# A two-transformer kernel on one core: the first transformer's query lengths moved from the queries to the score rows

## Chip, core and metric

One core of a Trainium2 chip runs the whole program. The metric is the time of one execution on the device in microseconds (us); the median of three runs is given, and beside it one execution that the hardware profiler recorded.

## What is computed

Four blocks in a row, each `x = x + s * silu(f)`, where `s` is an attention-like function and `f` a feed-forward-like function of the normalised `x`. The third block's `f` is a small transformer of six layers (below, the first transformer: 16 heads of 64, window 32); the fourth block's is another of two layers (8 heads, window 64). The tokens are 4 rows of 512, the width is 128, all in f32. Cut to what matters, a layer of the first transformer is:

```python
q, k, v = split(shift_tokens(x) @ Wqkv)          # 16 heads of 64
q = q / max(norm(q), 1e-12) * qs                 # per token and head
k = k / max(norm(k), 1e-12) * ksc
q = q * cos * scale + rotate_half(q) * sin * scale
k = k * cos / scale + rotate_half(k) * sin / scale
sim = einsum(q, k of this window and the one before) * 8, masked
x = softmax(sim) @ v @ Wo + x
x = feed_forward(layernorm(shift_tokens(x))) + x
```

The length of a query is one number per token and head. It can be applied to the query before the scores, or to the finished row of scores.

## The kernel before

Everything lies transposed: 128 channels on the partitions, tokens along the free axis. `_Transformer` runs three generators side by side, `queries_keys`, `attention` and `feed_forward`. The main loop (L724 to L732) takes one slot after the other; a slot is one batch row and one group of 8 heads, so the first transformer has 6 x 4 x 2 = 48 slots, and a few more to fill and drain. In a slot, `merge` (L949) takes turns between the generators by the costs that they yield (in us, written by hand: 10.3 for a slot of queries and keys, 20.4 for one of attention, 7.7 and 1.7 in turn for feed-forward). What comes out is then put in order on each engine by the framework's scheduler; each engine works through its own list in order.

**Queries and keys** (L1278). For queries (i = 0) and then keys (i = 1), and for two groups g of four heads, two 512-column products fill one PSUM tile S (L1300). From S come the squares (L1304, ScalarE), their sum over two halves (L1305, GpSimd), the two products with the rotation tables (L1306 and L1308, VectorE) and the sum of these (L1309, GpSimd). `unit_length` (L1319) sums the squares over a head by a product with a matrix of ones (L1326), takes Ln and Exp on ScalarE in place (L1329, L1330), and VectorE multiplies the rotated tile by the result (L1333, 128x1024, once per g). Eight DMAs on SP's queue (L1340) stack the tile by head pairs. Both queries and keys go through `unit_length`.

**Attention** (L1495) works on units: four heads (j = 0 or 1) of a slot's eight, all 512 tokens, so two units a slot. `values` (L1343) projects 64 tokens at a time into column halves (16 products of 256 columns a slot, L1358), copies them out of PSUM (L1365), and four DMAs (L1369, L1371) copy them to `ve`, shifted by a window for every other block. `scores` (L1383) writes the mask and adds 64 small products of 64 rows, 32 columns of weights and 64 moving columns (L1402), in two parts with the `turn` of the unit before in between. VectorE takes the maximum of each row (L1415) and subtracts it (L1419, two instructions), ScalarE takes the exponential (L1424), VectorE the row sums and their reciprocals (L1426, L1428). `turn` (L1431) transposes the exponentials (8 transpositions, copied by L1440). `weigh` (L1443) has 64 small products with the values, and VectorE divides by the row sums (L1473). `turn_back` (L1484) transposes the result (copies L1493), and four products with Wo (L1529) are added to the stream by L1533.

**Feed-forward** (L1543): layernorm (L1550 to L1559), products up (L1566, L1567), Gelu (L1569, with a load of its table), the gated product (L1571), products down (L1578). It takes two slots per row, so slots with the layernorm and the down products alternate with slots with the up products, roughly.

All of these share one PSUM pool of four S tiles (L715, `ps`), which is all of PSUM. A product into a tile waits until the last reader of the tile that had this place is done.

## Time and profile before

| | us |
|---|---|
| median of three runs | 3872.96 (3869.68 to 3877.02) |
| span of the profiled execution, first to last instruction | 3866.4 |
| first transformer in it | about 1640 to 3300 |
| TensorE busy in the span | 3490.9 |
| VectorE | 2476.9 |
| ScalarE | 1847.0 |
| GpSimd | 1161.2 |

For the profiled execution only its span is at hand, 6.6 us below the median of the runs. Engines are named PE (TensorE), PEld (its weight loads), DVE (VectorE), ACT (ScalarE), POOL (GpSimd), SPq (the DMA queue of SyncE). A group's line gives the source line, the engine, the operation, output and inputs with their shapes, the count, then busy time and mean ns of one, then the idle time before them and who ended it. A line of the timeline has start, duration, engine, line, operation and count, with the wait in brackets where there was one. A matrix product in f32 leaves two records. L122 and L126 are the helpers that issue products and transpositions, so groups under them are told apart by their tiles: `hb,l_wqk` is the query and key projection, `sqp,l_k` the product with ones, `hb,l_wv` or `l_wv,hb` the values, `l_v.,l_PT` the weighing, `l_OT,l_wo` the output projection, `core,l_P` and `core,l_On` the two transpositions.

### The profile page before, as it was taken

How to read it: one execution, taken by the hardware profiler on the slowest of the kernel's cores; microseconds unless marked ns; L12 is line 12 of the kernel's file. 1: busy time of each engine (PE TensorE's matmuls, PEld its weight loads, DVE VectorE, ACT ScalarE, POOL GpSimd, SP SyncE). 2: the span in 40 equal slices, each digit the busy share in tenths (PEclk: the TensorE clock that was granted, in tenths of full speed). 3: DMA queues.
4: the chain of work that ended last, by engine and by line, in shares of the span. 5: the costliest groups of instructions: out<-in, count | busy, mean ns of one | idle time of the engine just before them, and what ended most of it. 6: DMA issues, size and time to landing. Idle time of an engine off the chain costs nothing.

```text
span 3866.4 us, 105326 instructions
## 1 busy us (share of the span) xinstructions
PE 3490.9 (90%) x46789; PEld 1892.2 (49%) x46917; DVE 2476.9 (64%) x3429; ACT 1847.0 (48%) x2508; POOL 1161.2 (30%) x994
## 2 busy tenths in 40 slices
PE   6886999899899999899999999999999999778887
PEld 4554455444444443454555555555555555445444
DVE  6675555411553351677888888888888887367765
ACT  3333666623133334455555555555555555445555
POOL 1001344400021113443443443443443342042220
PEclk7677999999899999999999999999999999889998
DMA  1000000001000000444334444444444434322221
GB/s 39 8 24 24 8 1 1 1 30 52 2 1 3 3 1 2 116 99 117 95 94 122 96 96 120 95 99 117 98 99 103 103 88 98 110 63 69 53 49 42
DMA packets 123574, 236.12 MB, mean 61 GB/s; under 512 B 29624, under 2 KB 44128, under 8 KB 117728
## 3 DMA queue, kind: packets, MB, share of 16 engines
q1 hardware_dynamic: 114064, 209.58, 22.1%
q10 hardware_dynamic: 8624, 19.29, 1.6%
q8 instruction: 369, 6.05, 0.7%
q0 software_dynamic: 432, 0.51, 0.1%
q14 instruction: 85, 0.70, 0.1%
HBM read 50.08 MB, written 5.54 MB: 14 GB/s over the span
## 4 chain that ended last, share of the span: by engine, by line
PE 69%; ACT 11%; DVE 9%; issue 6%; DMA 2%; POOL 2%; SPq 0%; DVEq 0%; POOLq 0%; ACTq 0%
PE S L122 45%; PE S L126 6%; PE M L122 5%; PE S L1402 4%; PE o L1104 4%; ACT l_P L581 3%; PE o L614 2%; ACT l_PT L1440 1%; DMA l_tab<-in_k_rot_l 1%; PE S L1014 1%; DVE l_mx L1079 1%; ACT l_P L1126 1%; DVE l_rot L1333 1%; PE M L741 1%; DVE l_rot L1306 1%
## 5 line engine op out<-in xcount | busy, mean ns | idle before, releaser
L1309 POOL TENSOR_TENSOR l_rot<-l_rot,rotp 128x1024 f32<-128x1024 f32 x224 | 527.5, 2364 | 285.9 <-DVE rotp L1308 219.2
L1305 POOL TENSOR_TENSOR sqp<-sqp 128x512 f32<-128x512 f32 x224 | 293.3, 1310 | 832.8 <-ACT sqp L1304 825.6
L122 PE MATMUL S<-hb,l_wqk 128*128 128x512 f32 x896 | 449.4, 621 | 36.7 <-ACT l_PT L1440 11.2
L1304 ACT ACTIVATE sqp<-S 128x1024 f32<-128x1024 f32 x224 | 229.5, 1025 | 319.2 <-PE S L122 318.0
L1333 DVE SCALAR_TENSOR_TENSOR l_rot<-S,l_rot 128x1024 f32<-128x1024 f32 x224 | 262.9, 1211 | 65.3 <-ACT S L1330 37.4
L1306 DVE TENSOR_TENSOR l_rot<-S,l_tab 128x1024 f32<-128x1024 f32 x224 | 272.1, 1215 | 50.0 <-ACT sqp L1304 46.6
L126 PE MATMUL S<-core,l_P 128*128 128x128 f32 x1856 | 265.2, 287 | 38.9 <-ACT l_P L1424 16.4
L126 PEld LDWEIGHTS S<-core,l_P 128*128 128x128 f32 x1856 | 215.0, 146 | 136.8 <-issue 45.8
L122 PE MATMUL S<-l_KT,l_QT 32*128 32x256 f32 (+7 forms) x1536 | 247.4, 475 | 34.7 <-ACT l_P L1126 14.5
L1126 ACT ACTIVATE l_P<-S 128x1024 f32<-128x1024 f32 x160 | 156.8, 1023 | 254.9 <-PE S L122 254.1
L1308 DVE TENSOR_TENSOR rotp<-S,l_tab 128x1024 f32<-128x1024 f32 x224 | 270.5, 1208 | 1.4 <-POOL l_rot L1309 1.3
L122 PEld LDWEIGHTS S<-hb,l_wqk 128*128 128x128 f32 x896 | 158.3, 192 | 224.7 <-issue 151.6
L122 PE MATMUL S<-sqp,l_k 128*128 128x512 f32 x448 | 226.5, 623 | 19.1 <-issue 7.2
L1402 PE MATMUL S<-l_qk 64*32 64x64 f32 (+1 forms) x13312 | 221.1, 230 | 19.4 <-DMA l_qk<-l_rot 1.9
L1079 DVE TENSOR_REDUCE l_mx<-S 128x2 f32<-128x768 f32 (+1 forms) x192 | 154.9, 863 | 123.8 <-PE S L1014 123.8
L1402 PEld LDWEIGHTS S<-l_qk 64*32 64x32 f32 (+1 forms) x13312 | 168.2, 108 | 134.0 <-issue 129.6
L1130 POOL TENSOR_SCALAR_AFFINE_SELECT l_P<-l_P 128x256 f32<-128x256 f32 x256 | 99.8, 408 | 405.5 <-ACT l_P L1126 398.5
L122 PE MATMUL S<-l_wv,hb 128*64 128x256 f32 (+1 forms) x1600 | 219.1, 395 | 2.4 <-ACT l_vo L1365 1.2
L122 PE MATMUL S<-l_OT,l_wo 128*128 128x512 f32 (+1 forms) x512 | 207.1, 544 | 8.0 <-DVE ffu L1571 7.9
L1415 DVE TENSOR_REDUCE mx<-S 128x16 f32<-128x1024 f32 (+1 forms) x128 | 155.7, 1216 | 89.9 <-PE S L1402 89.8
L122 PE MATMUL S<-hb,l_w 128*128 128x512 f32 (+1 forms) x384 | 189.6, 630 | 23.5 <-DVE hb L1559 14.1
L122 PEld LDWEIGHTS S<-l_ve,l_PT 64*32 64x32 f32 (+1 forms) x6656 | 159.9, 108 | 99.2 <-issue 70.5
(360 smaller groups left out, 6544.8 us busy)
## 6 DMA issues: line engine op xcount, KB each, us to landing
l_qk<-l_rot SPq DMA_DIRECT2D x896, 128.0 KB
l_ve<-l_vo SPq DMA_DIRECT2D x112, 256.0 KB
l_ve<-l_vo SPq DMA_DIRECT2D x96, 224.0 KB
l_tab<-in_k_rot_l ACTq DMA_DIRECT2D x16, 1024.0 KB
l_wqk<-in_l2Wqkv SPq DMA_DIRECT2D x12, 512.0 KB
l_wv<-in_l2Wqkv SPq DMA_DIRECT2D x12, 256.0 KB
l_wo<-in_l2Wo SPq DMA_DIRECT2D x12, 256.0 KB
l_ve<-l_vo SPq DMA_DIRECT2D x24, 128.0 KB
```

The costliest lines, as they stand in the source:

```text
L122: self.nc.tensor.matmul(out, lhsT, rhs, start=start, stop=stop)
L126: self.nc.tensor.transpose(out, in_, self.ident[:n, :n])
L1079: nc.vector.tensor_reduce(mxv[:, bs, 2 * m + e, 3 - i], s[u][:, :, c : c + n], axis=AX.X, op=ALU.max)
L1126: nc.scalar.activation(P[u], s[u], AF.Exp, scale=scale)
L1304: nc.scalar.activation(sq, p, AF.Square)
L1305: nc.gpsimd.tensor_tensor(sq[:, 0, :], sq[:, 0, :], sq[:, 1, :], ALU.add)
L1306: nc.vector.tensor_tensor(t[:, g], p, tab[:, 0], ALU.mult)
L1308: nc.vector.tensor_tensor(m, p, tab[:, 1], ALU.mult)
L1309: nc.gpsimd.tensor_tensor(t[:, g], t[:, g], m[:, ::-1, :], ALU.add)
L1333: nc.vector.scalar_tensor_tensor(t[:, g], p[:, g, :].unsqueeze(1).to_broadcast([128, 2, S]), 1e12, t[:, g], ALU.min, ALU.mult)
L1402: net.nc.tensor.matmul(sv[W * bl : W * bl + W, e, t, g, :].rearrange("p (s k) -> p s k", s=2), qk[0][r, g, j, W * c : W * c + W], kw, star ...
L1415: nc.vector.tensor_reduce(mx, flat, axis=AX.X, op=ALU.max)
```

## The change

The first transformer (window 32) gets a class of its own, `_Paired`; the second keeps `_Transformer`.

- Keys are projected before queries. Keys still go through `unit_length`. Queries are stacked unscaled, right after their rotation.
- `lengths` sums the query squares on tokens: 32 products per slot, each with 128x32 squares as weights and 4 columns of the ones matrix moving, into a 128x32 result; Ln and Exp on that, and a small minimum on GpSimd.
- `weights_of`: maximum, one subtraction for the whole unit (128x1024), and then GpSimd multiplies the unit's rows by the query lengths; the exponential comes after that, in `exponentials`.
- The row sums and reciprocals move into `turn`, after the copy of the transposed exponentials.
- The 64 score products, and the 64 weighing products of the unit before, stand in one run each, with nothing yielded in between.
- Values are projected 128 tokens at a time over all 512 columns (4 products a slot); the blocks of a unit are numbered otherwise (c = 4(2t + bl/2) + 2a + bl%2), and the mask, the weights' column order and the copies to `ve` (again four DMAs) go with it.
- `turn_back` copies once (128x1024) in place of two halves, and the stream is added in two halves of 256 columns.
- A unit's order of work: its scores, weighing of the unit before, then values or output projection, then both transpositions; the attention weight of a slot is 16.1 in place of 20.4.

```diff
-            t = _Transformer(self, pre, heads, window, pools, consts)
+            t = (_Paired if window == 32 else _Transformer)(self, pre, heads, window, pools, consts)
...
-        self.attention_weight = 20.4 if self.split else 25.0
+        self.attention_weight = 16.1 if self.split else 25.0
...
+                for i in (1, 0):
...
+                        sq = self.TP.tile([128, 2, S], F32, name="sqp", bufs=3)
+                        nc.scalar.activation(sq, p, AF.Square)
+                        nc.gpsimd.tensor_tensor(sq[:, 0, :], sq[:, 0, :], sq[:, 1, :], ALU.add)
+                        nc.vector.tensor_tensor(t[:, g], p, tab[:, 0], ALU.mult)
+                        m = self.TP.tile([128, 2, S], F32, name="rotp", bufs=2)
+                        nc.vector.tensor_tensor(m, p, tab[:, 1], ALU.mult)
+                        nc.gpsimd.tensor_tensor(t[:, g], t[:, g], m[:, ::-1, :], ALU.add)
+                        sums.append(sq)
+                        if before:
+                            made["k"] = yield from self.unit_length(*before)
+                            before = None
+                    before = sums, t
+                made["q"] = self.stack(t)
+                made["r"] = yield from self.lengths(sums)
...
+    def lengths(self, sums):
+        net, nc = self.net, self.nc
+        p = self.M()[:, 0:32]
+        pv = p.rearrange("p (h n) -> p h n", h=4)
+        for t in range(2):
+            for g in range(2):
+                for a in range(2):
+                    for bl in range(4):
+                        c = 4 * (2 * t + bl // 2) + 2 * a + bl % 2
+                        net.mm(
+                            pv[32 * bl : 32 * bl + 32, :, 4 * t + 2 * g + a], sums[g][:, 0, 32 * c : 32 * c + 32], self.ones[:, ::32]
+                        )
+        yield 0.8
+        r = net.stat(32, "rq")
+        nc.scalar.activation(r, p, AF.Ln, bias=self.tiny)
+        nc.scalar.activation(r, r, AF.Exp, scale=-0.5)
+        nc.gpsimd.tensor_scalar(r, r, 1e12, None, ALU.min)
+        return r
...
+        for m in (0, 2):
+            p = self.S2()
+            for n in range(2):
+                net.mm(p[:, n, :], hb[:, 128 * (m + n) : 128 * (m + n) + 128], w)
+            yield 1.72
+            nc.scalar.copy(vo[:, m : m + 2, :], p)
+        for lo in (0, 64):
+            nc.sync.dma_start(ve[lo : lo + 32], vo[lo : lo + 32])
+        nc.sync.dma_start(ve[96:128], vo[32:64])
+        nc.sync.dma_start(ve[32:64, 1:4, :], vo[96:128, 0:3, :])
...
+    def weights_of(self, u, s, r):
+        net, nc = self.net, self.nc
+        mx = net.stat(16, "mx")
+        sv = s.rearrange("p e (n k) -> p (e n) k", k=64)
+        nc.vector.tensor_reduce(mx, sv, axis=AX.X, op=ALU.max)
+        P = u["P"] = self.PP.tile([128, 16, 64], F32, name=self.pre + "_P")
+        nc.vector.tensor_tensor(P, sv, mx.unsqueeze(2).to_broadcast([128, 16, 64]), ALU.subtract)
+        rq = r[:, 16 * u["j"] : 16 * u["j"] + 16]
+        nc.gpsimd.tensor_tensor(P, P, rq.unsqueeze(2).to_broadcast([128, 16, 64]), ALU.mult)
+
+    def exponentials(self, u):
+        self.nc.scalar.activation(u["P"], u["P"], AF.Exp, scale=8.0)
+
+    def turn(self, u):
...
+        u["PT"] = self.PP.tile([128, 8, 128], F32, name=self.pre + "_PT")
+        nc.scalar.copy(u["PT"], t)
+        rs = net.stat(16, "rs")
+        nc.vector.tensor_reduce(rs, P, axis=AX.X, op=ALU.add)
+        u["r"] = net.stat(16, "r")
+        nc.vector.reciprocal(u["r"], rs)
...
+            if u:
+                if i % 2 == 0:
+                    qk = self.made.pop((u["l"], u["b"], u["gp"]))
+                else:
+                    u["ve"], u["vo"] = last["ve"], last["vo"]
+                s = self.scores(qk, u["j"])
+            if last:
+                o = self.weigh(last)
+            if u:
+                self.weights_of(u, s, qk["r"])
+            if last:
+                self.divide(last, o)
+            if u or last:
+                yield 2.8
+            behind = None
+            if i % 2 == 0 and i + 2 < len(units):
+                behind = self.values(units[i + 2])
+            elif i % 2 and i > 2:
+                behind = self.close(units[i - 2], OT.pop(i - 2))
+            if behind:
+                yield next(behind)
+            if u:
+                self.exponentials(u)
+            if behind:
+                yield from behind
+            if last:
+                if i % 2:
+                    made = self.TP.tile([128, 4, S], F32, name=self.pre + "_OT", bufs=1)
+                else:
+                    OT[i - 1] = made
+                self.turn_back(last, made)
+                yield 0.9
+            if u:
+                self.turn(u)
+                yield 0.9
```

More of the change, by code (lines that the diff above doesn't have):

```diff
@@ L1201, in __init__ @@
         nc.vector.tensor_copy(self.identb, net.ident)
-        self.ve = [C.tile([128, self.NU, 1024 // self.NB], F32, name=f"{pre}_ve{i}") for i in range(2)]
-        for i in range(2 if self.split else 1):
+        self.ve = [C.tile([128, 4 if self.split else 2, 512], F32, name=f"{pre}_ve{i}") for i in range(2)]
+        if not self.split:
             for lo, hi in self.second():
-                nc.gpsimd.memset(self.ve[i][lo:hi, 0, :], 0.0)
+                nc.gpsimd.memset(self.ve[0][lo:hi, 0, :], 0.0)
         self.made, self.shift, self.weights = {}, {}, {}
-        self.attention_weight = 20.4 if self.split else 25.0
+        self.attention_weight = 16.1 if self.split else 25.0
         self.feed_forward_weights = (7.7, 1.7) if self.GP == 2 else (9.4,)
@@ L1335, in unit_length, with stack @@
             )
+        return self.stack(t)
+    def stack(self, t):
+        nc = self.nc
         out = self.QK.tile([128, 2, 2, S], F32, name=self.pre + "_qk")
@@ L1581, in feed_forward, with __init__, queries_keys, values @@
             yield None
+class _Paired(_Transformer):
+    def __init__(self, *args):
+        super().__init__(*args)
+        for ve in self.ve:
+            self.nc.gpsimd.memset(ve[32:64, 0, :], 0.0)
+    def queries_keys(self, rows):
+        net, nc = self.net, self.nc
+        for l, b in rows:
+            hb = net.shifted(net.tok(self.y, b), self.TP, 3)
+            self.shift[l, b] = hb
+            hk = hb.rearrange("p (u s k) -> p s u k", s=2, k=self.W)
+            for gp in range(self.GP):
+                w = self.part("qk", l, gp)
+                before, made = None, {}
+                for i in (1, 0):
+                    tab = self.tables(l, i)
+                    t = self.TP.tile([128, 2, 2, S], F32, name=self.pre + "_rot", bufs=2)
+                    sums = []
+                    for g in range(2):
+                        p = self.S2()
+                        for h in range(2):
+                            c = 128 * (4 * g + 2 * i + h)
+                            o = p[:, h, :]
+                            net.mm(
+                                o.rearrange("p (s u k) -> p s u k", s=2, k=self.W) if i else o, w[:, c : c + 128],
+                                hk if i else hb,
+                            )
[14 more added lines that the diff above has]
+                made["r"] = yield from self.lengths(sums)
+                self.made[l, b, gp] = made
+                yield None
+    def lengths(self, sums):
[3 more added lines that the diff above has]
+        for t in range(2):
+            for g in range(2):
+                for a in range(2):
+                    for bl in range(4):
+                        c = 4 * (2 * t + bl // 2) + 2 * a + bl % 2
+                        net.mm(
+                            pv[32 * bl : 32 * bl + 32, :, 4 * t + 2 * g + a], sums[g][:, 0, 32 * c : 32 * c + 32], self.ones[:, ::32]
+                        )
+        yield 0.8
[4 more added lines that the diff above has]
+        return r
+    def values(self, u):
+        net, nc = self.net, self.nc
+        w, hb = self.part("v", u["l"], u["gp"]), self.shift[u["l"], u["b"]]
+        ve = u["ve"] = self.ve[u["gp"]]
+        vo = u["vo"] = self.VP.tile([128, 4, 512], F32, name=self.pre + "_vo")
+        for m in (0, 2):
+            p = self.S2()
+            for n in range(2):
+                net.mm(p[:, n, :], hb[:, 128 * (m + n) : 128 * (m + n) + 128], w)
+            yield 1.72
+            nc.scalar.copy(vo[:, m : m + 2, :], p)
[3 more added lines that the diff above has]
+        nc.sync.dma_start(ve[32:64, 1:4, :], vo[96:128, 0:3, :])
+    def scores(self, qk, j):
+        net, nc = self.net, self.nc
+        s = self.S2()
+        for e in range(2):
+            net.mm(s[:, e, :], self.identb, self.mask[:, 0, :])
+        sv = s.rearrange("p e (t g a s k) -> p e t g a s k", t=2, g=2, a=2, s=2)
+        for t in range(2):
+            for g in range(2):
+                for a in range(2):
+                    for bl in range(4):
+                        c = 4 * (2 * t + bl // 2) + 2 * a + bl % 2
+                        k0, step = self.window(c)
+                        for e in range(2):
+                            r = slice(64 * e, 64 * e + 64)
+                            kt = qk["k"][r, g, j, :]
+                            kw = bass.AP(kt.tensor, kt.offset + k0, [list(kt.ap[0]), [step, 2], [1, 32]])
+                            nc.tensor.matmul(
+                                sv[32 * bl : 32 * bl + 32, e, t, g, a], qk["q"][r, g, j, 32 * c : 32 * c + 32], kw,
+                                start=False, stop=True, skip_group_check=True, tile_position=(r.start, 32 * bl),
+                            )
+        return s
+    def weights_of(self, u, s, r):
+        net, nc = self.net, self.nc
+        mx = net.stat(16, "mx")
[8 more added lines that the diff above has]
+    def turn(self, u):
+        net, nc = self.net, self.nc
+        P = u["P"]
+        t = self.S2().rearrange("p a (b q) -> p (a b) q", q=128)
+        for i in range(8):
+            net.transpose(t[:, i, :], P[:, 2 * i : 2 * i + 2, :].rearrange("p a k -> p (a k)"))
+        u["PT"] = self.PP.tile([128, 8, 128], F32, name=self.pre + "_PT")
[4 more added lines that the diff above has]
+        nc.vector.reciprocal(u["r"], rs)
+    def weigh(self, u):
+        net = self.net
+        PT, vo, ve, j = (u[k] for k in ("PT", "vo", "ve", "j"))
+        o = self.S2()
+        for t in range(2):
+            for g in range(2):
+                for e in range(2):
+                    d = 64 * (4 * g + 2 * j + e)
+                    x = 64 * (4 * t + 2 * g + e)
+                    for bl in range(4):
+                        v = vo if bl % 2 else ve
+                        for a in range(2):
+                            r = slice(64 * a, 64 * a + 64)
+                            net.mm(
+                                o[32 * bl : 32 * bl + 32, a, x : x + 64], PT[r, 4 * e + 2 * t + g, 32 * bl : 32 * bl + 32],
+                                v[r, 2 * t + bl // 2, d : d + 64],
+                            )
+        return o
+    def divide(self, u, o):
+        On = u["On"] = self.PP.tile([128, 2, 4, 2, 64], F32, name=self.pre + "_On", bufs=1)
+        rv = u["r"].rearrange("p (e n a) -> p a n e", e=2, a=2)
+        for a in range(2):
+            self.nc.vector.tensor_tensor(
+                On[:, a], o[:, a, :].rearrange("p (n e d) -> p n e d", e=2, d=64),
+                rv[:, a].unsqueeze(3).to_broadcast([128, 4, 2, 64]), ALU.mult,
+            )
+    def turn_back(self, u, OT):
+        net = self.net
+        t = self.S2().rearrange("p g (x q) -> p g x q", q=128)
+        for g in range(2):
+            for th in range(2):
+                for a in range(2):
+                    net.transpose(t[:, g, 2 * th + a, :], u["On"][:, a, 2 * th + g].rearrange("p e d -> p (e d)"))
+        ov = OT.rearrange("p (g j) n -> p j g n", j=2)
+        self.nc.scalar.copy(ov[:, u["j"]], t.rearrange("p g x q -> p g (x q)"))
+    def close(self, u, OT):
+        net, nc = self.net, self.nc
+        wo = self.part("o", u["l"], u["gp"])
+        p = self.M()
+        for t in range(4):
+            net.mm(p, wo[:, t, :], OT[:, t, :], t == 0, t == 3)
+            if t % 2:
+                yield 1.72
+        y = net.tok(self.y, u["b"]).rearrange("p (t m a x) -> p t m a x", t=2, m=2, a=2)
+        p = p.rearrange("p (t a m x) -> p t m a x", t=2, m=2, a=2)
+        for t in range(2):
+            nc.vector.tensor_tensor(y[:, t], y[:, t], p[:, t], ALU.add)
+    def attention(self, rows):
+        units = [dict(l=l, b=b, gp=gp, j=j) for l, b in rows for gp in range(2) for j in range(2)]
+        yield from self.values(units[0])
+        OT = {}
+        for i in range(len(units) + 2):
+            if i % 2:
+                yield None
+            u = units[i] if i < len(units) else None
+            last = units[i - 1] if 0 < i <= len(units) else None
+            if u:
[24 more added lines that the diff above has]
+            if last:
+                if i % 2:
+                    made = self.TP.tile([128, 4, S], F32, name=self.pre + "_OT", bufs=1)
[6 more added lines that the diff above has]
+                yield 0.9
@@ L1611, in _constants @@
         j = np.arange(w)[None]
-        mask = np.zeros((128, NT, 2, 2, w), f)
-        for q in range(NT):
+        mask = np.zeros((128, 2, 2, 2, 2, w) if w == 32 else (128, NT, 2, 2, w), f)
+        for q in range(2 if w == 32 else NT):
             for blk in range(128 // w):
@@ L1616, in _constants @@
                 own, before = (0, 1) if blk % 2 == 0 else (1, 0)
-                mask[rows, q, :, own] = np.where(j <= i, 0.0, MASKED)[rows][:, None]
-                seen = (j >= i) & (q + blk > 0)
-                mask[rows, q, :, before] = np.where(seen, 0.0, MASKED)[rows][:, None]
+                mask[rows, q, ..., own, :] = np.where(j <= i, 0.0, MASKED)[rows].reshape((w,) + (1,) * (mask.ndim - 4) + (w,))
+                seen = np.where(j >= i, 0.0, MASKED)[rows]
+                mask[rows, q, ..., before, :] = seen.reshape((w,) + (1,) * (mask.ndim - 4) + (w,))
+        first = mask[0:w, 0, :, 0] if w == 32 else mask[0:w, 0]
+        first[..., 1, :] = MASKED
         c["k_" + name] = np.concatenate([ones, cen, mask.reshape(128, -1)], 1)
@@ L1655, in _columns, with _halves @@
     return np.stack(out, 1)
-def _halves(w, heads, even_first):
+def _halves(w, heads):
     n = heads * 64
@@ L1668, in _halves @@
                 order.append((i * n + (4 * g + r) * 64 + 32 * half + d).reshape(-1))
-    v = 2 * n + np.arange(n).reshape(heads // 8, 8, 64)
-    for part in v:
-        order += [part[0::2].reshape(-1), part[1::2].reshape(-1)] if even_first else [part.reshape(-1)]
+    order.append(2 * n + np.arange(n))
     return w[:, :, np.concatenate(order)]
@@ L1700, in _layout @@
             a[pre + dst] = i[src + n]
-        a[pre + "Wqkv"] = _halves(a[pre + "Wqkv"], (L2F if pre == "l2" else L3F)["heads"], pre == "l2")
+        a[pre + "Wqkv"] = _halves(a[pre + "Wqkv"], (L2F if pre == "l2" else L3F)["heads"])
         a[pre + "cols"] = _columns(*(i[src + n] for n in ("q_scale", "k_scale", "ln_g", "ln_b", "b1", "b2")))
```

## The prediction

> **What bounds the kernel now.** I read the page's busy shares and slices first, then the stage table, then who ended TensorE's idle time, then TensorE's pieces in order of time.

> The page, parts 1 and 2, whose span is 3866.4 us:

> ```profile
> PE 3490.9 (90%) x46789; PEld 1892.2 (49%) x46917; DVE 2476.9 (64%) x3429; ACT 1847.0 (48%) x2508; POOL 1161.2 (30%) x994
> ...
> PE   6886999899899999899999999999999999778887
> ```

> The stretch of nines from slice 18 to 33 is the first transformer, the only stage that the change touches (about 1640 to 3300 us). One piece of it in the stage table (columns: length, then busy time of PE, PEld, DVE, ACT, POOL, then clock):

> ```profile
> 2260.00:2482.00 222.00, 211.27 (x3756) 116.49 (x3766) 183.19 (x199) 119.28 (x136) 89.29 (x55) 0.99 0.44 108
> ```

> TensorE is busy 95% of it, VectorE 83%, GpSimd 40%. The waits that ended TensorE's idle time from 1834 to 3127 us are short (total, times, longest):

> ```profile
> PE S L122 <- ACT l_PT L1440: 8.1, 18, 0.5
> PE S L126 <- DVE ffu L1571: 7.6, 18, 0.4
> ```

> So TensorE bounds the stage: the other engines hand it tiles almost in time. In the chain that ended last (start, length, what) the long pieces that end in a weighing run come once a slot; every second one:

> ```profile
> 1905.50 12.62 PE S L122 x128
> ...
> 1976.52 12.62 PE S L122 x128
> ```

> The next ones stand at 2047.53, and 2121.50 to 2192.51: two slots of the main loop take 71.0 to 71.1 us (once a layer some 3 us more). I reckon with 71.05.

> **The work that goes.** The price of a TensorE piece is the time from its start to the next piece's start:

> ```profile
> 2305.66 0.25 PE L122 MATMUL S<-l_ve,l_PT 64*32 64x64 f32 x2
> ...
> 2307.08 1.95 PE L122 MATMUL S<-l_wv,hb 128*64 128x256 f32 x16
> 2308.95 1.98 PE L122 MATMUL S<-sqp,l_k 128*128 128x512 f32 x4
> 2310.78 0.38 PE L122 MATMUL S<-l_mask,l_identb 128*128 128x512 bf16 x1
> 2311.30 0.86 PE L1402 MATMUL S<-l_qk 64*32 64x64 f32 x64
> 2312.09 1.09 PE L126 MATMUL S<-core,l_P 128*128 128x128 f32 x8
> ...
> 2325.60 3.70 PE L122 MATMUL S<-hb,l_w 128*128 128x512 f32 x8
> ```

> The 128 records of a whole weighing run take 1.42 us; half a score run 0.79; a ones product pair 1.83; eight value products 1.87; four 512-column products 3.64 (the piece after the last line starts at 2329.24; an f32 product is two records). Per slot:
> - query lengths: one ones pair of two goes, -1.83;
> - 32 narrow length products (64 records of 128*32, 4 columns) come. The nearest rows are these, 18 columns wide:

> ```profile
> 86.64 0.20 PE L122 MATMUL M<-l_ve,l_PT 128*32 128x18 f32 x1
> ...
> 86.74 0.18 PE L122 MATMUL M<-l_vo,l_PT 128*32 128x18 f32 x1
> 86.75 0.18 PE L122 MATMUL M<-l_ve,l_PT 128*32 128x18 f32 x1
> ```

> They follow each other by 8 to 9 ns at a granted clock of 1.00 (86 to 88 us); the 64 of this run, until the next piece at 87.31, take 0.67 us. I take that: +0.67. Columns are not what counts in it: 128 records of one column (L741, 32*32) run from 24.0 to 25.1 us, 8.6 ns each, so from below I set 64 x 8.6 = 0.55. From above, 64 records of 128 columns with weights of the same size (on xn, from 1321.79) last 1.95.
> - values: two eights, 3.74, become four 512-column products, 3.64: -0.10;
> - scores: two units in halves, 4 x 0.79, become two runs at 1.45: -0.26; weighing: one unit of two stood in halves, 1.58 becomes 1.41: -0.17.

> Sum -1.7 us a slot, -3.4 a pair. Work in a pair was 68.1 us with such prices, so waits were 2.9 of 71.05.

> [...]

> **The work that comes.** GpSimd multiplies each unit's 128x1024 score rows by the lengths. The trace has the same operation, with a broadcast second operand, elsewhere:

> ```profile
> L595 POOL TENSOR_TENSOR l_P<-l_P,l_r 128x1024 f32<-128x1024 f32 x48 | 90.9, 1895 | 66.6 <-DVE l_r L586 56.0 <-PE S L126 10.6
> L1309 POOL TENSOR_TENSOR l_rot<-l_rot,rotp 128x1024 f32<-128x1024 f32 x224 | 527.5, 2364 | 285.9 <-DVE rotp L1308 219.2 <-DMA l_ve<-l_vo 62.2 <-DMA l_qk<-l_rot 4.4
> ```

> I take 1.9 us (bounds: 1.31, the 512-element sum L1305, and 2.36). Twice a slot that is 3.8 us on an engine busy 40%: as load it is free. As a link it is not: it stands between subtraction and exponential, and ScalarE and VectorE keep their order, so what is queued behind the exponential and the row sums waits too; on GpSimd itself a rotation addition (L1309, 2.36) stands behind each multiply, and the query stack waits for that in the values half. VectorE gains 2.4 us a slot (two L1333 of 1.21 go), ScalarE 2.1 (L1329, L1330). Those are hidden behind TensorE.

> In the order of the built program I followed one pair by hand, zero at the end of a unit's scores, durations from the rows: maximum 1.22, subtraction 1.21, multiply 1.9, exponential 1.05, rotation product 1.13, Square 1.02, PSUM copy 1.01. Each S tile takes one of four PSUM places and must wait for its last reader there.
> - Values half: one rotation product stands between maximum and subtraction. Subtraction ends at 3.6, and the next projection, which takes the scores' place, starts at 3.65 instead of 3.25: 0.4. Multiply ends 5.55, exponential 6.65; behind it on ScalarE the key lengths' Exp, a Square and the first values copy end at 9.75. The length products take that tile's place, and TensorE is there at 9.1: 0.7.
> - The same half with the feed-forward output (2.67 us more of TensorE): 0.4 + 0.2, the rest is covered.
> - Projection half with the feed-forward input: exponential ends 5.6, then table load 1.28, Gelu 0.69 and its product 0.75 give up a place at 8.4, wanted at 6.85: 1.6.
> - Projection half with the layernorm: row sums wait for the exponential at 5.6, two rotation products end at 9.1; their place is wanted at 7.85: 1.3. Two smaller ones, 0.25 and 0.5.

> Sum 5.35 us a pair where it was 2.9 (nothing is added for small gaps, which these longer ones cover). A pair becomes 68.1 - 3.4 + 5.35 = 70.05 us, 1.0 less.

> Keys first and queries unscaled move the query stack's eight DMAs ahead by the length of L1329 to L1333. SP's queue now has four value copies, then eight key pieces, then eight query pieces; before, eight such issues took some 6.6 us (2326.3 to 2332.9). Begun at 11, they end near 28, and the scores read them at about 32: 4 us of cover, and without it the scores wait for the difference. The y addition in two halves and the smaller statistics are 0.2 us a slot on engines with room: nothing.

> **Sum.** 48 slots, some 46 at full pace, 23 pairs: work -3.4 x 23 = -78 us, waits +2.45 x 23 = +56, together -22. Span 3866.4 - 22 = 3844; the median of the runs stands 6.6 us above the profiled span, so **3851 us**.

> **Rivals.**
> - The waits stay at 2.9 us a pair, because TensorE runs ahead less than I reckon or the exponentials find gaps. Then the whole -78 arrives: 3795. For it: the waits shown above are at most 0.5 us. Against: no GpSimd link is in the chain now.
> - The multiply is the bound of the half: at L1309's 2.36 us it puts 0.46 on four waits of each pair, 0.46 x 4 x 23 = +42, 3893. It decides from 1.9 + 22/(4 x 23) = 2.14 us, beyond which the kernel is slower than before. For it: L1309 and L595 are both GpSimd products of 1024 elements and differ by a quarter; more GpSimd time also meets VectorE's copies (L89 takes from 0.38 to 2.19 us in this trace). Against: L595 has the like operands.
> - The change does not make lengths cheaper: narrow products at the 128-column row, 1.95 - 0.67 = 1.28 us more a slot. They stand on TensorE behind a wait and nothing covers them: 1.28 x 46 = +59, 3910. The 8.6 ns of the one-column rows speak against it; for it, that those are 32 rows deep and these 128, and that no row has 4 columns.

> **Chances.** 0.2% is 7.7 us, about what a measurement can tell from no change. Forecast 0.44 (3835 to 3870: 0.37 of it faster, 0.07 within); waits stay 0.18, faster; multiply 0.28 (0.24 slower, 0.04 within, as it may lie between 1.9 and 2.36); lengths 0.10, slower. Together faster 0.55, same 0.11, slower 0.34. The range takes in the first rival, and of the slower side the multiply and most of the lengths: 3792 to 3906. The lower bound of the multiply, 1.31, would take 0.59 x 4 x 23 = 54 off, 3797, which lies inside.

> **What would show it.** A pair of slots in 70.0 us; length runs of 0.6 to 0.8 us; the multiply at 1.9; TensorE's idle time ended by the values copy, the Gelu product and a rotation product, each 0.5 to 1.7 us. Wrong if those waits are missing (first rival), if the multiply is over 2.14 us, or if scores wait for a DMA into l_qk.

## The result, and the profile after

The changed kernel takes **4046.63 us** (median of four runs, 4042.2 to 4050.12) where the kernel before takes 3874.99 beside it: 1.0443 times as long, 95% interval 1.0417 to 1.0469. The profiled execution has a span of 4044.8 us, 178.4 more than before. The whole difference lies in the first transformer: from its first projection to its last weighing product it takes 1909.8 us (1567.0 to 3476.8) where it took 1731.7 (1566.4 to 3298.1).

The page after, parts 1 and 2 (busy time of TensorE, its slices, the clock it was granted):

```profile
PE 3453.5 (85%) x48517; PEld 1911.5 (47%) x48645; DVE 2374.0 (59%) x3285; ACT 1748.8 (43%) x2412; POOL 1355.4 (34%) x1136
...
PE   7887999899899998887888888888888788778887
PEclk7677999999999989998999999999999899889999
```

TensorE is busy 37 us less in the span, but the nines of slices 18 to 33 have become eights, with two sevens. Who ended its idle time, after and then before (both 1834 to 3300 us; total, times, longest):

```profile
PE S L122 <- issue: 151.4, 74, 6.2
PE S L122 <- DMA l_wqk<-in_l2Wqkv: 27.8, 2, 20.5
PE S L122 <- DMA l_wv<-in_l2Wqkv: 11.4, 1, 11.4
PE S L1686 <- issue: 9.9, 7, 2.0
PE S L122 <- ACT l_vo L1664: 6.0, 7, 2.2
```
```profile
PE S L122 <- issue: 8.6, 19, 1.3
```

Neither GpSimd nor a VectorE product is at the top. "Issue" means that TensorE waited for nothing that the profile shows. The timeline of one unit shows where it sits, in the middle of a weighing run (L122, `l_PT`), behind a score run that started at 2429.79:

```profile
2431.84 0.23 PE L122 MATMUL S<-l_vo,l_PT 64*32 64x64 f32 x2
2431.87 0.23 PE L122 MATMUL S<-l_ve,l_PT 64*32 64x64 f32 x2
2434.26 0.25 PE L122 MATMUL S<-l_vo,l_PT 64*32 64x64 f32 x2 [2.16 <-issue]
...
2435.04 3.35 PE L122 MATMUL S<-sqp,l_k 128*128 128x512 f32 x4
2438.22 1.88 PE L122 MATMUL S<-hb,l_wqk 128*128 128x512 f32 x4
```

Two things are to be seen. The weighing products on both sides of the gap have the same operands and results; nothing arrives between them. And the ones pair behind the gap lasts 3.2 us to the next piece instead of 1.83. The stage table says why (length, then busy time of PE, PEld, DVE, ACT, POOL, then the clock):

```profile
2425.00:2430.00 5.00, 4.85 (x52) 3.08 (x56) 4.75 (x6) 2.45 (x4) 4.69 (x3) 1.00 0.00 0
2430.00:2435.00 5.00, 2.84 (x256) 2.55 (x236) 4.94 (x4) 0.56 (x1) 2.83 (x2) 0.94 0.02 3
2435.00:2440.00 5.00, 5.00 (x16) 2.22 (x10) 2.68 (x4) 1.53 (x2) 4.15 (x2) 0.72 0.02 5
```

The granted clock was 1.00 ahead of the gap and 0.72 behind it (read more finely: 0.50 from 2434.4 to 2437.8, then 1.00 again). Over the stage it was 1.00 before the change and is 0.94 after, in the same table:

```profile
1640.00:3310.00 1670.00, 1590.81 (x28985) 883.21 (x29078) 1366.35 (x1491) 898.32 (x1020) 672.22 (x409) 1.00 0.42 103
```
```profile
1640.00:3490.00 1850.00, 1554.85 (x30629) 900.71 (x30722) 1270.53 (x1359) 803.07 (x924) 862.23 (x549) 0.94 0.39 93
```

What TensorE runs out of can be read from the DMA queues. Before and after (packets, MB, share):

```profile
q8 instruction: 369, 6.05, 0.7%
```
```profile
q8 instruction: 383, 6.28, 0.7%
```

From first projection to last weighing, TensorE's idle time is, in us (sums of the waits in its timeline):

| ended by | before | after |
|---|---|---|
| nothing named ("issue") | 12 | 204 |
| a DMA (weights, one stack) | 0 | 45 |
| another engine | 66 | 43 |

Together +214 us. The stage grew by 178, so TensorE's pieces gave back 36, where the forecast had 78. The lowered clock is part of that. It stands at 0.50 for 239 us of this stage (20 before), 45 of them idle. If work at 0.50 takes up to twice as long, as the ones pair nearly did (3.2 us for 1.83, most of it at 0.50), half of the other 194 us is lost, some 80 to 90 us more than before. That is an estimate; by it the pieces would have given back about 120 at the full clock, more than the forecast's 78.

### The profile page after: what moved, and what is told of

It reads as the page before. It is cut to its first block, busy times and chain, and to the rows that moved or that the text cites. A ratio compares the mean times of both kernels' runs of the same rounds, so it can differ in the third digit from the quotient of the medians.

```text
span 4044.8 us, 108642 instructions
## 1 busy us (share of the span) xinstructions
PE 3453.5 (85%) x48517; PEld 1911.5 (47%) x48645; DVE 2374.0 (59%) x3285; ACT 1748.8 (43%) x2412; POOL 1355.4 (34%) x1136
## 4 chain that ended last, share of the span: by engine, by line
PE 63%; issue 10%; DVE 10%; ACT 9%; POOL 3%; DMA 3%; SPq 2%; POOLq 0%; DVEq 0%; ACTq 0%
PE S L122 40%; PE S L126 5%; PE M L122 5%; PE o L1104 3%; PE S L1686 3%; ACT l_P L581 3%; PE o L614 2%; SPq L1344 1%; PE S L1014 1%; DVE l_mx L1079 1%; ACT sqp L1619 1%; ACT l_P L1126 1%; DVE l_rot L1621 1%; PE M L741 1%; PE S L1406 1%
## 5 line engine op out<-in xcount | busy, mean ns | idle before, releaser
L1624 POOL TENSOR_TENSOR l_rot<-l_rot,rotp 128x1024 f32<-128x1024 f32 x192 | 456.1, 2383 | 192.8 <-DVE rotp L1623 182.3
L122 PE MATMUL S<-hb,l_wqk 128*128 128x512 f32 x896 | 459.4, 633 | 44.0 <-DMA l_wqk<-in_l2Wqkv 27.8
L1620 POOL TENSOR_TENSOR sqp<-sqp 128x512 f32<-128x512 f32 x192 | 248.7, 1295 | 372.4 <-ACT sqp L1619 347.5
L126 PE MATMUL S<-core,l_P 128*128 128x128 f32 x1856 | 264.1, 287 | 45.5 <-ACT l_P L1428 17.2
L122 PE MATMUL S<-l_ve,l_PT 64*32 64x64 f32 (+1 forms) x6656 | 213.8, 232 | 100.0 <-issue 90.5
L122 PEld LDWEIGHTS S<-hb,l_wqk 128*128 128x128 f32 x896 | 175.0, 205 | 252.4 <-issue 214.6
L1621 DVE TENSOR_TENSOR l_rot<-S,l_tab 128x1024 f32<-128x1024 f32 x192 | 233.7, 1217 | 96.7 <-ACT sqp L1619 75.5
L122 PE MATMUL S<-l_vo,l_PT 64*32 64x64 f32 (+1 forms) x6656 | 210.5, 233 | 93.0 <-issue 93.0
L1703 ACT ACTIVATE l_P<-l_P 128x1024 f32<-128x1024 f32 x96 | 101.3, 1055 | 423.1 <-POOL l_P L1700 420.2
L122 PE MATMUL S<-l_KT,l_QT 32*128 32x256 f32 (+7 forms) x1536 | 247.4, 475 | 34.7 <-ACT l_P L1126 14.5
L126 PEld LDWEIGHTS S<-core,l_P 128*128 128x128 f32 x1856 | 217.1, 147 | 116.0 <-issue 29.7
L1700 POOL TENSOR_TENSOR l_P<-l_P,rq 128x1024 f32<-128x1024 f32 x96 | 182.5, 1902 | 262.1 <-DVE l_P L1698 234.8
L122 PEld LDWEIGHTS S<-l_ve,l_PT 64*32 64x32 f32 (+1 forms) x6656 | 175.6, 111 | 131.2 <-issue 114.5
L122 PE MATMUL S<-l_wv,hb 128*128 128x512 f32 x448 | 214.2, 609 | 19.2 <-DMA l_wv<-in_l2Wqkv 11.4
L122 PEld LDWEIGHTS S<-l_vo,l_PT 64*32 64x32 f32 (+1 forms) x6656 | 171.5, 111 | 97.6 <-issue 97.3
L1696 DVE TENSOR_REDUCE mx<-S 128x16 f32<-128x1024 f32 x96 | 117.2, 1221 | 169.8 <-PE S L1686 169.5
L122 PE MATMUL S<-l_OT,l_wo 128*128 128x512 f32 (+1 forms) x512 | 207.3, 544 | 7.7 <-DVE ffu L1575 7.7
```

What stands on the lines that cost most here:

```text
L122: self.nc.tensor.matmul(out, lhsT, rhs, start=start, stop=stop)
L126: self.nc.tensor.transpose(out, in_, self.ident[:n, :n])
L1620: nc.gpsimd.tensor_tensor(sq[:, 0, :], sq[:, 0, :], sq[:, 1, :], ALU.add)
L1621: nc.vector.tensor_tensor(t[:, g], p, tab[:, 0], ALU.mult)
L1624: nc.gpsimd.tensor_tensor(t[:, g], t[:, g], m[:, ::-1, :], ALU.add)
L1700: nc.gpsimd.tensor_tensor(P, P, rq.unsqueeze(2).to_broadcast([128, 16, 64]), ALU.mult)
```

## Theory and rivals

**Fetch theory:** instructions reach TensorE in blocks of 256 (254 recorded ones a packet, as counted above), and a new block is fetched only when one has been used up (the bursts below bear on this). In the kernel before, the packets come 4 to 17 us apart (2255 to 2344 us); a block of narrow products alone lasts 1.4 (1.42 us for a whole weighing run there). When the next block is needed sooner than its fetch takes, TensorE stands (2.16 us in the gap above), and the clock may fall (to 0.50 behind it). **Chain theory:** the forecast's own, that the GpSimd multiply and what queues behind it hold TensorE. **Weights:** the loads for the next layer, which now stand late on SP's queue, cost time of their own.

## Experiments

**More work between the runs.** Six mask products are written into the weighing tile and overwritten.

```diff
         o = self.S2()
+        for k in range(6):
+            net.mm(o[:, k % 2, :], self.identb, self.mask[:, 0, :])
```

> The changed kernel with six more 512-column bf16 mask products written into the weighing tile ahead of each weighing run (the weighing overwrites them). A pair of mask products has a pitch of 0.52 us in the profile after, so this adds 1.56 us of TensorE work to each of 96 units, 150 us in all. Fetch theory (TensorE runs out of instructions inside the 512 instructions of a score run and a weighing run, because each block of 256 arrives some 3.6 us after the block before the last is entered): the gap shrinks by what the filler takes, and the half clock that follows a gap of 2 us goes too: 3990 to 4060 us, no slower than the changed kernel's 4047. Chain theory (the multiply on GpSimd and what is queued behind it holds TensorE) or any theory in which TensorE's own work counts: 4150 to 4200 us.

Measured: 4016.55 us, 1.0388 of before (1.0368 to 1.0408). The added products take 1.40 us a unit in the trace, some 135 us in all (the expectation had 150), and yet the kernel became some 20 us faster by the ratios. TensorE's waits, 1640 to 3480 us:

```profile
PE S L122 <- issue: 63.1, 85, 3.9
PE S L122 <- ACT l_vo L1664: 57.1, 25, 3.4
```

In the same stretch the changed kernel has 189.7 us of "issue" on L122, and the mean clock of the stage rose from 0.94 to 0.98. TensorE's own work does not bound the stage, then. But work put into idle time is free whatever ends that time: the run shows where the loss sits, not yet what it is.

**Useful work between them.** The first half of the values or of the output projection goes between scores and weighing.

```diff
                 s = self.scores(qk, u["j"])
-            if last:
-                o = self.weigh(last)
-            if u:
                 self.weights_of(u, s, qk["r"])
-            if last:
-                self.divide(last, o)
-            if u or last:
-                yield 2.8
+                yield 1.4
             behind = None
...
             if behind:
                 yield next(behind)
+            if last:
+                o = self.weigh(last)
+                self.divide(last, o)
+                yield 1.4
```

> The changed kernel with the first half of the values or of the output projection (and what else falls there, 3.6 to 7 us of wide products) between the score run and the weighing run of a unit. Nothing else is changed. Fetch theory: no block of 256 instructions is left that lasts under 3.6 us, the gaps in the weighing run go (the trace after shows 182 us of them in the stage) and with them the half clock: 3800 to 3880 us, so about the price on record for the change without this loss. Chain theory: the waits are where they were, 4000 to 4060 us.

Measured: 3988.58 us (1.0305, 1.0286 to 1.0325), outside both ranges. Most of the gaps went, as expected ("issue" 37.7 us with the scores' share, where the changed kernel has 201.7), but 57.5 us of waits for `l_wqk`, 56.4 for the rotation products and 42.2 for the divided output (L1741) took their place. In this order the weighing comes late in the unit, and the transposition behind it waits for the divided output. So the edit moved more than the gap. A better placed one follows below.

**No multiply.**

```diff
-        nc.gpsimd.tensor_tensor(P, P, rq.unsqueeze(2).to_broadcast([128, 16, 64]), ALU.mult)
```

> The changed kernel without the GpSimd multiply of the score rows (the query lengths are then not applied). Fetch theory: the exponential comes 1.9 us earlier, which nothing on the path waits for: 4025 to 4050 us. Chain theory: the multiply is the link that holds TensorE, and its 1.9 us come back on most of the 96 units: 3870 to 3930 us.

Here the query lengths are not applied. Measured: 4031.24 us (1.0406, 1.0376 to 1.0436), inside the fetch theory's range and far from the chain theory's. "Issue" is still 184 us (1640 to 3480 us; 202 in the changed kernel). Waits for `l_wqk` are 78.3 us, 50 more than in the changed kernel, so part of what the multiply held up may be lost there again; this run alone does not price the multiply.

**Narrow products by themselves.** Five bursts ahead of the transformer, in the kernel before.

```diff
+            if pre == "l2":
+                for n in (64, 128, 256, 512, 1024):
+                    wide = t.S2()
+                    for i in range(8):
+                        self.mm(wide[:, i % 2, :], t.ones, self.tok(self.xn, 0))
+                    narrow = t.S2()
+                    for i in range(n):
+                        a, bl, x = i % 2, 32 * (i // 2 % 4), 64 * (i // 8 % 8)
+                        r = slice(64 * a, 64 * a + 64)
+                        self.mm(narrow[bl : bl + 32, a, x : x + 64], t.ones[r, 0:32], t.cen[r, 0:64])
```

> The kernel before with five runs of nothing but narrow products (64 rows, 32 columns of weights, 64 moving columns, f32) put ahead of the first transformer: 64, 128, 256, 512 and 1024 products, with eight 512-column f32 products ahead of each; nobody reads them. A product is four instructions of TensorE, so the runs are 1, 2, 4, 8 and 16 blocks of 256 instructions. Fetch theory: the first two blocks run at 1.4 us a block, every further one takes some 3.6 us: about 1.4, 3 to 5, 10, 24 and 53 us, with gaps that stand 256 instructions apart. If narrow products have no such limit: 1.4, 2.8, 5.7, 11.4 and 22.7 us, without gaps.

The burst of 1024 products, in the timeline (the last column is the wait ahead):

```profile
1654.32 1.84 PE L122 MATMUL S<-l_k 64*32 64x64 f32 x128 [2.05 <-issue]
1658.07 2.04 PE L122 MATMUL S<-l_k 64*32 64x64 f32 x128 [1.91 <-issue]
1661.81 2.04 PE L122 MATMUL S<-l_k 64*32 64x64 f32 x128 [1.70 <-issue]
1665.57 2.05 PE L122 MATMUL S<-l_k 64*32 64x64 f32 x128 [1.71 <-issue]
1669.06 2.04 PE L122 MATMUL S<-l_k 64*32 64x64 f32 x128 [1.44 <-issue]
```

128 records with their 128 weight loads, then a gap, again and again: 256 instructions every 3.47 to 3.76 us. The DMA queues and the stage table for 1654 to 1706 us:

```profile
q8 instruction: 14, 0.23, 1.8%
```
```profile
1654.00:1706.00 52.00, 29.22 (x1836) 25.69 (x1835) 0.00 (x0) 0.00 (x0) 0.00 (x0) 0.51 0.02 4
```

One packet of 16 KB per group, nothing else on the DMA engines, no other engine at work. The groups took 3.5 us although the clock had fallen to 0.51 and half of that time was work: the fetch sets the pace, not TensorE. In one period of the trace TensorE goes on at 1597.06, the next packet starts at 1598.19 and ends at 1599.45, and TensorE goes on with it at 1600.80.

From start to the next wide product the five bursts took 1.4, 2.7, 12.4, 26.6 and some 56 us. The one of 64 products has no gap, nor has that of 128 (512 instructions): by the count of instructions it happens to begin with a block, so that both of its blocks were there. The first pieces of the three longer ones, up to their first gap:

```profile
1592.22 2.63 PE L122 MATMUL S<-l_k 64*32 64x64 f32 x244
```
```profile
1614.60 2.45 PE L122 MATMUL S<-l_k 64*32 64x64 f32 x228
```
```profile
1649.95 2.32 PE L122 MATMUL S<-l_k 64*32 64x64 f32 x212
```

That is 212 to 244 records, 424 to 488 instructions: about two blocks are in store, no more. This carries the fetch theory by itself.

**The same in the kernel before.** Both transpositions go ahead of the scores, and the weighing follows them at once; and, as a control, the same with wide products between.

```diff
+            if last and self.split:
+                yield from self.turn(last)
+            if older and self.split:
...
+                self.turn_back(older, OT)
+                yield 0.9
             if u:
...
                 u["P"], u["r"] = yield from self.scores(qk, u["tp"], u["j"], last)
...
+            if last and self.split:
+                yield from self.weigh(last)
+                yield 2.8
```

In both, `scores` and `weigh` yield nothing on the way. In the control the weighing stays behind the output projection, as in the kernel before, and these lines stand between it and the scores:

```diff
+            if u and self.split:
+                yield 2.8 if i % 2 else 5.6
```

> The kernel before with its scores of a unit and the weighing of the unit before in one run each, one behind the other, so 512 narrow instructions in a row as in the changed kernel (both transpositions go ahead of the scores; lengths, values and exponentials stay as they are). Fetch theory: each of 96 units loses some 2 us in the run and some of the half clock behind it, and the halves' small gains come back: 3990 to 4090 us, with gaps of TensorE inside the weighing run that nothing ends. Chain theory (GpSimd's multiply, which this kernel does not have): 3850 to 3920 us.

> The same edit of the kernel before, with wide products between the score run and the weighing run; a control for the moved transpositions. Fetch theory: no gaps without a name inside the weighing runs, and 100 us or more below the joined kernel: 3840 to 3930 us. If it was the new order and not the unbroken run that cost the time in the joined kernel, the two are within 40 us of each other.

Measured: joined 4123.51 us (1.0629, 1.0603 to 1.0655), apart 3934.21 (1.0145, 1.012 to 1.017). The kernel before, which has no multiply and no narrow lengths, loses 248 us when its runs are joined, more than expected, and 189 of them come back with wide work between. The control is 4 us above its expected range, and it is not free of gaps: 43 us of "issue" are left (26.9 on L122, 15.8 in the score runs). The joined kernel's waits, 1640 to 3480 us:

```profile
PE S L122 <- issue: 214.4, 92, 3.6
PE S L122 <- DMA l_wqk<-in_l2Wqkv: 16.5, 1, 16.5
```

92 gaps for 96 units. The control stays 59 us above the kernel before, mostly in waits for the divided output (39.8 us) and the sum of squares (27.6): what the order of before was good for.

**Weights early.** SP's queue at the first layer change, before and after (start, length):

```profile
1794.16 0.54 SPq L1239 DMA_DIRECT2D l_wqk<-in_l2Wqkv  x1
...
1812.60 19.73 SPq L1340 DMA_DIRECT2D l_qk<-l_rot  x16
```
```profile
1833.35 13.76 SPq L1344 DMA_DIRECT2D l_qk<-l_rot  x16
1847.21 1.49 SPq L1666 DMA_DIRECT2D l_ve<-l_vo  x2
...
1850.11 0.92 SPq L1239 DMA_DIRECT2D l_wqk<-in_l2Wqkv  x1
```

Before, the first load stands ahead of the stack; after, behind it, and TensorE waits for it until 1855.53, 20.47 us. The edit issues it ahead again:

```diff
+                if b == B - 1 and (l + 1, 0) in rows:
+                    self.part("qk", l + 1, gp)
                 made["q"] = self.stack(t)
...
+        if u["b"] == B - 1 and u["l"] + 1 < 6:
+            self.part("v", u["l"] + 1, u["gp"])
```

> The changed kernel, but with the next layer's projection weights (queries and keys, values) issued on SP's queue ahead of the stacks of the slot that reads the old ones last, where the changed kernel has them behind these stacks. The trace after has three waits for these loads, 20.5, 11.4 and 7.3 us, 39 us in all, and the half clock that follows the first. If these waits are a cause of their own beside the fetch: 3990 to 4020 us. If they only take the place of other waits: 4035 to 4060 us.

Measured: 4031.45 us (1.0398, 1.0373 to 1.0424). The waits for these weights are gone, but 18.4 us of waits for the output weights (`l_wo`) appear, and "issue" on L122 is 201.5 us, 12 more than in the changed kernel. Of 39 us some 15 came back, which lies between the two expected ranges. The two intervals of the ratios overlap a little, though none of these runs (4022.79 to 4039.05) is as long as the shortest of the changed kernel (4042.2). It is a smaller cause of its own, part of which only changes places.

**Both mended.** The yield goes between scores and weighing (the weighing keeps its place ahead of the values), weights early as above.

```diff
                 s = self.scores(qk, u["j"])
+                self.weights_of(u, s, qk["r"])
+                yield 1.4
             if last:
                 o = self.weigh(last)
-            if u:
-                self.weights_of(u, s, qk["r"])
-            if last:
                 self.divide(last, o)
-            if u or last:
-                yield 2.8
+                yield 1.4
```

> The changed kernel with a yield between the score run and the weighing run of a unit (which puts one piece of wide products there, 0.9 to 2.7 us, against 3.6 to 7 us in the first split), and with the weights early. Fetch theory with the weights as second cause: blocks of 256 instructions then last 2.3 us or more, so gaps of 0 to 1.4 us stay, and 57 us of waits for weights that the first split had go: 3850 to 3930 us. If the first split's 3989 us were the chain behind the multiply, it stays above 3960.

Measured: 3880.67 us (1.0013, 0.9992 to 1.0034), inside the expected range and 166 below the changed kernel. The weights alone gave some 15 of these, so the yield gave most of them. What is left, 1640 to 3340 us:

```profile
PE S L122 <- issue: 37.3, 37, 3.3
PE S L122 <- DVE ffu L1575: 23.4, 11, 3.0
PE S L122 <- DMA l_wo<-in_l2Wo: 21.1, 5, 5.3
PE S L1690 <- issue: 15.2, 13, 2.1
```

**More wide work between, and two terms of the forecast on top of it.** The yields become 2.8 and 0.3, the output weights go early too. From this version one kernel drops the multiply, another takes the query lengths as before.

```diff
-                made["q"] = self.stack(t)
-                made["r"] = yield from self.lengths(sums)
+                made["q"] = yield from self.unit_length(sums, t)
+                made["r"] = None
...
-        rq = r[:, 16 * u["j"] : 16 * u["j"] + 16]
-        nc.gpsimd.tensor_tensor(P, P, rq.unsqueeze(2).to_broadcast([128, 16, 64]), ALU.mult)
```

> The changed kernel with a longer yield behind the scores (2.8, then 0.3 behind the weighing), so that four 512-column products at least (1.8 us of wide work) stand between every score run and weighing run, and with the next layer's output weights early too, beside those of the projections. Fetch theory: a block that holds the wide piece lasts 1.42 + 1.82 us or more, so the 52 us of gaps of the version before it shrink to under 20, their half clock with them, and its 21 us of waits for the output weights go: 3790 to 3845 us, faster than the kernel before. If the remaining loss was the chain behind the multiply: 3865 to 3900 us.

> The version with wide products between, without the GpSimd multiply of the score rows (the query lengths are then not applied). The forecast on record put 2.45 us of waits a pair on the multiply and what queues behind it, 56 us in all: if that holds once the fetch is out of the way, this is 30 to 60 us below the version with it. If TensorE's own work bounds the stage, under 15 us.

> The version with wide products between, but with the queries' lengths taken and applied as in the kernel before (a second pair of ones products, Ln and Exp over 1024 columns, two more VectorE products; no narrow length products, no multiply of score rows). By the forecast's prices TensorE works 1.16 us more a slot, 56 us in all, and the multiply's waits of 56 us go: within 25 us of the version with the new lengths. If the multiply costs nothing: 35 to 60 us above it.

Measured: 3855.57 us (twelve runs, 3836.99 to 3881.59; 0.9954, 0.9931 to 0.9977), half a per cent below the kernel before; without the multiply 3820.35 (0.9854, 0.9831 to 0.9876); with the old lengths 3908.89 (1.0088, 1.0066 to 1.011). The first is some 10 us above the upper end of its expected range. Its profiled execution is the longest of the twelve, and there the gaps, expected under 20 us, are 53:

```profile
PE S L122 <- issue: 39.0, 21, 3.5
PE S L122 <- DVE ffu L1575: 27.3, 15, 2.4
PE S L1690 <- issue: 14.2, 16, 2.0
```

A weighing run alone is still 256 instructions, and can be a whole block; one that starts at 2356.59 stands for 2.01 us ahead of its last five records, although TensorE had waited 1.63 us ahead of it. The kernel before has such runs too, and 12 us of gaps. That halves with wide work between would remove the rest was not tried.

The two variants price the forecast's terms with the fetch mostly out of the way. The multiply costs 35 us, within its expectation (each of the ratios is known to about 9 us). The old lengths, which need no multiply, are 88 us dearer than the new ones without it, and 53 dearer than the new ones with it: in this arrangement the idea of the change is worth 53 us net. By the forecast's prices the two were to lie within 25 us of each other. The 53 fall into the range that was named for a multiply that costs nothing, but the run without it shows that it does cost: it is the gain of the lengths that the forecast had too small.

**Fetch under traffic.** The long gaps of the changed kernel (6.18 us at 2174.3) stand beside a stack and a table load. The bursts again, with 48 copies of the stacks' kind started at the last burst:

```diff
...
+                        for k in range(6):
+                            out = t.QK.tile([128, 2, 2, S], F32, name="l2_qk")
+                            for r in range(4):
+                                for h in range(2):
+                                    x = 32 * (2 * (r % 2) + h)
+                                    self.nc.sync.dma_start(out[x : x + 32, :, r // 2, :], rot[32 * r : 32 * r + 32, :, h, :])
```

> The five bursts of narrow products once more, now with 48 copies of the kind of the query and key stacks (128 KB each, from one tile to others that nobody reads) on SP's queue, started with the burst of 1024 products. In the bursts without traffic each 256 instructions took 3.47 to 3.76 us. In the trace after, the longest gaps (5 to 6 us) stand where a stack and a table load were in flight. If an instruction fetch waits among other transfers: 4.5 to 6 us a block while the copies run, and 3.5 again after them. If those long gaps were something else: 3.5 to 3.8 throughout.

```profile
1659.57 1.61 PE L122 MATMUL S<-l_k 64*32 64x64 f32 x128 [2.01 <-issue]
1663.86 2.04 PE L122 MATMUL S<-l_k 64*32 64x64 f32 x128 [2.68 <-issue]
1667.88 2.05 PE L122 MATMUL S<-l_k 64*32 64x64 f32 x128 [1.97 <-issue]
1671.92 2.04 PE L122 MATMUL S<-l_k 64*32 64x64 f32 x128 [1.99 <-issue]
```

4.0 to 4.6 us a block while the copies run (to 1697), 3.5 to 4.0 after them. That lies between the two expectations: traffic of this kind adds about half a microsecond. The packets themselves are hardly longer (1.15 us at the median, 1.04 without the copies); the half microsecond passes before they start (1.65 us from where TensorE goes on to the start of the next packet, against 1.13). The changed kernel has two "issue" gaps over 2.8 us, of 5.0 and 6.18. There too the packet comes late: in the gap of 6.18 it starts 3.36 us after TensorE has stopped, and then takes 1.34. What holds it back that long stays open.

## Why the prediction was wrong

**The step that failed** is in the work: "scores: two units in halves, 4 x 0.79, become two runs at 1.45: -0.26; weighing: one unit of two stood in halves, 1.58 becomes 1.41". The score run is right: 1.29 to 1.49 us in 2400 to 2545 us, median 1.39. The weighing run, in the same stretch, takes 2.43 to 7.03 us, about 4 at the median; over the stage the weighing products, with the gaps in them, take 362 us where they took 162. The price of 1.41 came from a row of before in which a run of 256 instructions stood alone between wide products. It was carried to a place where 512 stand in a row, and there the row's surroundings, which had hidden the fetch (packets 4 to 17 us apart, 12 us of "issue" in the stage), were gone. The forecast counted this join as a gain of 0.43 us a slot. Its one term of idle time, +56 us of waits behind the multiply, was answered by +214 us, 192 of them in gaps that end with nothing named.

- **TensorE bounds the stage:** right as far as the other engines go, which hardly make it wait. But for 204 us of the stage it stands with nothing named, and the forecast has no term for that.
- **Work, -78 us:** 36 arrived. By the estimate above it was about 120 at the full clock, and the lowered clock, which the forecast has no term for, took some 80 to 90 of it.
- **Narrow lengths, 0.67 us a run:** right; median 0.71, and not the 1.95 of the rival.
- **Values 3.64:** right, 3.53 where the four stand in one piece.
- **Multiply 1.9 us:** right; 1902 ns in the group of L1700:

```profile
L1700 POOL TENSOR_TENSOR l_P<-l_P,rq 128x1024 f32<-128x1024 f32 x96 | 182.5, 1902 | 262.1 <-DVE l_P L1698 234.8
```

- **Waits of 5.35 us a pair behind it:** not seen in the changed kernel, where the gaps cover them (other engines end 43 us, less than before). With the gaps mostly out of the way the multiply costs 35 us, where the forecast added 56: right in kind, too large.
- **The lengths' gain of 1.16 us a slot,** 56 us in all: 88 us between the kernels with old and new lengths without a multiply. That comparison includes what ScalarE and VectorE are spared, which the forecast set at nothing: with the old lengths TensorE waits 36.2 us for VectorE's product with them (L1333), with the new ones, where that product is left for the keys alone, 8.5.
- **SP's queue:** the 4 us of cover for the stacks held but once (one wait, of 5.4 us). That the same queue carries the next layer's weights was missed: 39 us of waits, some 15 of them at stake.
- **Rivals:** none named the supply of instructions. That 3851 and the 3855.57 of the mended version are close is partly luck, as that version still has 53 us of gaps, and a mean clock of 0.97 in the stage.

## What to carry to other kernels

Count TensorE's instructions, not only their time: an f32 product was four, and where 256 in a row took 1.4 us at full clock, a new block came only every 3.47 to 3.76 us (the bursts). TensorE stood for the difference ("issue", in the middle of a run), behind some of the gaps it went on at a lowered clock (0.50 behind the gap at 2432), and with wide products in between most of this went ("issue" on L122 from 189.7 to 37.3 us, both mended). A piece's price holds for its neighbourhood: before two pieces are joined, ask what the work between them was hiding. Where a change moves stores or stacks on a queue, list everything else that this queue carries, the next layer's weights too.

## What the hardware showed beyond this

The clock fell after some of the gaps of about 2 us: behind the gap of 2.16 us it was 0.72 over the next 5 us, and the ones pair took 3.2 us instead of 1.83. Of the stage's 41 gaps of 2.0 to 2.5 us, 21 were followed by a fall of the clock within 3.5 us; of the 12 gaps of 1.0 to 1.5 us, two.

In a long burst, narrow products follow each other at 27 to 29 ns on the mean (128 records in 3.47 to 3.76 us), but not evenly: some 11 ns inside a block at full clock (1.42 us for 128), then a gap. The 8 to 9 ns of the prediction's rows were read from a run of 64 records, 128 instructions, which is half a block.
